# The order of the last batch's layer matrix, outputs and gates in a residual-stack kernel, and its last rows in two PSUM banks

## Chip, cores and metric

The kernel runs on one core of a Trainium2 chip. The metric is the device time of one execution in microseconds (us). Five engines work side by side and meet through semaphores: PE (TensorE, with PEld for its weight loads), DVE (VectorE), ACT (ScalarE), POOL (GpSimd) and SP (SyncE, which issues most DMAs). In the trace each engine's instructions come in the order in which the built program holds them.

## What is computed

`x` has 16 batches of 512 steps with 512 features. Four layers are added to it one after the other:

```python
x = x + L0(x, cond)   # a gate per batch: x becomes g2 * x
x = x + L1(x, cond)   # an RNN over the 512 steps
x = x + L2(x, cond)   # two sigmoid gates f, i and a candidate c; then
                      #   f, i <- f/(f+i), i/(f+i); scans along the steps
x = x + L3(x, cond)   # x @ (base + A_b B_b^T): one matrix for each batch b
```

L2 needs, for each batch, three products `x @ W` (512 x 512 each), a reciprocal, and three scans over the 512 steps. L3 needs for each batch a matrix `layer` of 512 x 512, made of a base and a product of rank 8 (with the identity of the residual folded into the base), and then the product of the batch's L2 result with it.

## The kernel before

The RNN comes first (to about 912 us of the span) and holds PE with thousands of small matmuls; in its shadow a part of the L2 gates is made early and parked in DRAM (`early`). What the change touches is the second stage, the loop over the batches `b` from line 758 on, with features on the partitions in four chunks `j`:

- `gate_unit(b, j, x3)` (L684 to L720) makes one chunk of the L2 result. PE makes `pf`, `pi`, `pc` (L684, each four matmuls 128x128 by 128x(512-te), te being the steps that were made early; the trace shows each of these float32 matmuls as two, so x8). ACT takes sigmoids of `pf` and `pi` (L699). DVE then runs ten instructions: the sum L700, the reciprocal L701, L702 to L705, the scans L709, L713 and L715, and the product L712. POOL adds the rest (L719, L720) into `x3`; for the very last chunk DVE does these two itself. PSUM holds one bank for `pf`, one for `pi`, and two for `pc` (`pc0`, `pc1`, by j). The SBUF tiles `f`, `i`, `s` have two buffers each, so ACT can write `f` of chunk j+1 only when POOL's L719 has read `f` of chunk j-1.
- `layer_of(b, ...)` makes the matrix of L3 in four banks, `pl0`, `pl1`, `po0`, `po1`: four matmuls with 8 rows (L525), and four DVE additions of the base (L529), which free the four banks. Its result goes to `wx_sb`, in the last batch to `base_sb` itself.
- `last_layer(b, x3, layer)` makes the outputs: four row tiles t, each of four matmuls 128x128 by 128x512 (L739) into `po0` or `po1` in turn, a copy by ACT (L734) and a DMA issued by SP (L735).

For b up to 14 the calls come as gates j = 0, 1, then the outputs of batch b-1, then gate j = 2, the matrix of batch b, gate j = 3. For b = 15 the matrix is called after gate j = 0, and the outputs of batch 14 after gate j = 3. Then come the outputs of batch 15: four banks `pl0`, `pl1`, `po0`, `po1` collect the chunks k = 0 to 2 first, which need no result of the last gate chunk, and then k = 3. The last row tile's bank is copied in two halves, by ACT and by DVE, which leave by two DMAs, issued by SP and ACT.

The order in this stage isn't written out by hand: the framework's scheduler places the instructions of every engine from the order of the calls and its own estimates. A tile's new owner waits until the engines that used the old one are done with it.

Of the kernel before, what the change touches and what calls it, by code (L numbers as in the profile page):

```python
# [30 lines left out]
F32 = mybir.dt.float32  # L31
# [4 lines left out]
P = 128  # L36
B, S, D = 16, 512, 512
KC = D // P
# [45 lines left out]
def kernel(  # L84
# [21 lines left out]
    nc = tc.nc  # L106
# [19 lines left out]
    base_sb = keep.tile([P, KC, D], F32)  # L126
# [387 lines left out]
    def load_layer(b, at, bt):  # L514
        for c in range(KC):
            rows = slice(c * BP, c * BP + R)
            nc.sync.dma_start(out=at[rows, :], in_=factor[0][b, :, c * P : (c + 1) * P])
            nc.sync.dma_start(out=bt[rows, :], in_=factor[1][b])
        return at, bt

    def make_layer(at, bt, banks):

        for c, pl in enumerate(banks):
            rows = slice(c * BP, c * BP + R)
            nc.tensor.matmul(pl, at[rows, :], bt[rows, :], start=True, stop=True)  # L525

    def add_base(banks, layer):
        for c, pl in enumerate(banks):
            nc.vector.tensor_tensor(layer[:, c, :], pl, base_sb[:, c, :], ALU.add)  # L529
# [25 lines left out]
    for n in range(NBLK):  # L555
# [3 lines left out]
        for s in range(T):  # L559
# [35 lines left out]
            bank, place = PLACE[g]  # L595
            for c in range(KC):
                at = slice(c * BP, (c + 1) * BP)
# [9 lines left out]
            if s == max(PAIRS[g]):  # L607
                t0, t1 = PAIRS[g]
                step = t1 - t0
                at = slice(n * T + t0, n * T + t1 + step // abs(step), step)  # L610
# [11 lines left out]
            if s in (2, 6) and n < 2 * KC:  # L622


                i = 2 * n + s // 6
                if i < 3 * KC:
                    m, which = divmod(i, 3)
                    w_sb, w = ((wf_sb, wfT), (wi_sb, wiT), (wc_sb, wcT))[which]
                    j = (KC - 2, KC - 1, 0, 1)[m]
                    at = slice(j * P, (j + 1) * P)  # L630
                    nc.scalar.dma_start(out=w_sb[:, :, at], in_=chunks(w)[:, :, at])
                else:
                    k = i - 3 * KC
# [19 lines left out]
        if n == NBLK - 4:  # L653
            at = w2pool.tile([P, P], F32, tag="b2", name="at_0", bufs=2)
# [10 lines left out]
    work = ctx.enter_context(tc.tile_pool(name="work", bufs=2))  # L665
# [9 lines left out]
    def bank(tag, name):  # L675
        return pools[tag].tile([P, D], F32, tag=tag, name=f"{tag}_{name}")
# [45 lines left out]
    def layer_rows(b):  # L722
        at = work.tile([P, P], F32, tag="at", name=f"at_{b}", bufs=1)
        bt = work.tile([P, D], F32, tag="bt", name=f"bt_{b}", bufs=1)
        return load_layer(b, at, bt)

    def layer_of(b, at, bt, layer):
        banks = [bank(tag, f"{b}_layer") for tag in ("pl0", "pl1", "po0", "po1")]
        make_layer(at, bt, banks)
        add_base(banks, layer)  # L730

    def leave(b, t, po, tag="osb"):
        osb = work.tile([P, D], F32, tag=tag, name=f"osb_{b}_{t}")
        nc.scalar.copy(osb, po)  # L734
        nc.sync.dma_start(out=out[b, t * P : (t + 1) * P, :], in_=osb)  # L735

    def output_part(po, t, x3, layer, ks):
        for k in ks:
            nc.tensor.matmul(  # L739
                po, x3[:, k, t * P : (t + 1) * P], layer[:, k, :], start=(k == 0), stop=(k == KC - 1)  # L740
            )

    def last_layer(b, x3, layer):
        for t in range(S // P):
            po = bank(f"po{t % 2}", f"{b}_{t}")
            output_part(po, t, x3, layer, range(KC))
            leave(b, t, po)

    layer = wx_sb
    pending = None  # L750
    for b in range(B):
        x3 = x3pool.tile([P, KC, S], F32, tag="x3", name=f"x3_{b}")
        end = b == B - 1
        if 0 < b < B - 1:
            factors = layer_rows(b)
        for j in range(KC):
            gate_unit(b, j, x3)
            if j == (KC - 1 if end else 1) and pending is not None:
                last_layer(*pending)
            if j == 2 and 0 < b < B - 1:  # L760
                layer_of(b, *factors, layer)
            if j == 0 and end:

                layer_of(B - 1, *layer_rows(B - 1), base_sb)
        pending = b, x3, layer

    pos = [bank(tag, "last") for tag in ("pl0", "pl1", "po0", "po1")]
    for t, po in enumerate(pos):
        output_part(po, t, x3, base_sb, range(KC - 1))
    for t, po in enumerate(pos):  # L770
        output_part(po, t, x3, base_sb, (KC - 1,))

        tag = ("osb", "f", "i", "s")[t]
        if t < KC - 1:
            leave(B - 1, t, po, tag)

    osb = work.tile([P, D], F32, tag=tag, name="osb_last")
    for n, copy in enumerate((nc.scalar.copy, nc.vector.tensor_copy)):
        at = slice(n * D // 2, (n + 1) * D // 2)
        copy(osb[:, at], pos[-1][:, at])  # L780
        (nc.sync, nc.scalar)[n].dma_start(out=out[B - 1, (KC - 1) * P :, at], in_=osb[:, at])


# [56 lines left out]
```

## Time and profile before

| | |
|---|---|
| median of 3 runs | 1621.4 us (1620.3 to 1623.64) |
| the profiled execution, its own time | 1621.03 us |
| its span, first to last instruction | 1619.2 us |
| PE busy | 1607.0 us, 99% of the span |
| DVE busy | 1132.3 us, 70% |
| ACT busy | 421.5 us, 26% |
| POOL busy | 172.9 us, 11% |
| mean granted clock of PE | 0.999 |

The page of the profile shows one execution. All times below are microseconds from the start of its span. A line of the timeline reads: start, duration, engine, line of the kernel, operation, output tile <- input tiles, shapes, count, and in brackets how long the engine stood idle before it and who released it. Tile names are shown without their numbers, so `s` or `pf` is that of whatever chunk is due at that time; the chunk is found by the order and by the width (the early part differs by chunk: for batch 15, 320 columns are left in chunks 0 and 1, 368 in chunk 2, 352 in chunk 3).

### The profile page before, as it was taken

To read this page: it belongs to the slowest core of one execution; us is meant where nothing else is said; L and a number is where in the kernel's file an instruction comes from. 1 tells how busy PE (TensorE), PEld (TensorE's weight loads), DVE (VectorE), ACT (ScalarE), POOL (GpSimd) and SP (SyncE) were. 2 spreads that over 40 slices of the span, in tenths; PEclk is the share of its full clock that TensorE was granted. 3 is DMA by queue.
4 is the path that set the end of the run, shared out by engine and by line. 5 is a ranking of instruction groups with operands and counts; after the bars stand their busy time and mean duration, and the time that the engine had idled before them with its cause. 6 is when DMAs were issued, how large, how long until landed. Compare 5 with 4: busy or idle time off the path is not lost.

```text
span 1619.2 us, 67613 instructions
## 1 busy us (share of the span) xinstructions
PE 1607.0 (99%) x29319; PEld 1147.3 (71%) x29320; DVE 1132.3 (70%) x3618; ACT 421.5 (26%) x2484; POOL 172.9 (11%) x145
## 2 busy tenths in 40 slices
PE   8999999999999999999999999999999999999998
PEld 6888888888888888888888655555555555555564
DVE  3555655665665666656665798888888888998887
ACT  3333333333333333333333211111111111111111
POOL 1000000000000000000000022221222222222212
PEclk9999999999999999999999999999999999999999
DMA  6555432111111111111111001111111111111111
GB/s 211 137 153 134 120 106 60 31 37 37 37 36 37 37 36 37 36 34 33 37 38 31 26 23 35 40 43 39 43 39 42 44 46 39 31 44 46 41 41 60
DMA packets 117683, 88.09 MB, mean 54 GB/s; under 512 B 20949, under 2 KB 97529, under 8 KB 117385
## 3 DMA queue, kind: packets, MB, share of 16 engines
q1 hardware_dynamic: 77968, 63.43, 13.0%
q10 hardware_dynamic: 39416, 20.34, 4.4%
q8 instruction: 229, 3.75, 1.0%
q14 instruction: 70, 0.57, 0.1%
HBM read 55.67 MB, written 28.07 MB: 52 GB/s over the span
## 4 chain that ended last, share of the span: by engine, by line
PE 96%; DVE 1%; DMA 1%; issue 1%; ACT 0%; POOL 0%; SPq 0%; ACTq 0%; POOLq 0%; DVEq 0%
PE pre L407 41%; PE po L739 13%; PE pg L455 13%; PE pf L684 9%; PE pi L684 9%; PE pc L684 9%; PE pf L370 1%; PE pl_layer L525 1%; DMA xb<-in_xT_dram 1%; PE po_last L739 0%; PE pl_last L739 0%; DMA wx_sb<-in_wx_dram 0%; DVE s L701 0%; POOL s L719 0%; DVE s L709 0%
## 5 line engine op out<-in xcount | busy, mean ns | idle before, releaser
L407 PEld LDWEIGHTS pre<-wh_sb,h_out 128*32 128x32 f32 x16384 | 469.2, 110 | 146.4 <-DVE h_out L599 141.7
L407 PE MATMUL pre<-wh_sb,h_out 128*32 128x128 f32 x16384 | 569.6, 273 | 3.1 <-DVE h_out L599 1.1
L599 DVE STREAM_TRANSPOSE h_out<-a 128x32 f32<-128x32 f32 x2048 | 264.7, 186 | 352.5 <-ACT a L598 351.4
L598 ACT ACTIVATE a<-pre 128x32 f32<-128x32 f32 x2048 | 238.2, 203 | 579.7 <-PE pre L407 579.5
L407 PE MATMUL pre<-wx_sb,x 128*32 128x128 f32 x8192 | 292.0, 273 | 1.2 <-DMA wx_sb<-in_wx_dram 1.1
L407 PEld LDWEIGHTS pre<-wx_sb,x 128*32 128x32 f32 x8192 | 244.3, 110 | 3.0 <-DMA wx_sb<-in_wx_dram 1.5
L739 PE MATMUL po<-wx_sb,x 128*128 128x512 f32 x480 | 208.7, 592 | 0.0
L739 PEld LDWEIGHTS po<-wx_sb,x 128*128 128x128 f32 x480 | 91.1, 190 | 111.2 <-issue 105.5
L684 PE MATMUL pf<-x,wf_sb 128*128 128x352 f32 (+3 forms) x512 | 165.5, 466 | 1.9 <-ACT f L699 1.5
L684 PE MATMUL pi<-x,wi_sb 128*128 128x352 f32 (+3 forms) x512 | 163.6, 462 | 0.0
L684 PE MATMUL pc<-x,wc_sb 128*128 128x352 f32 (+3 forms) x512 | 163.6, 462 | 0.0
L701 DVE RECIPROCAL s<-s 128x368 f32<-128x368 f32 (+2 forms) x64 | 152.2, 2378 | 2.2
L684 PEld LDWEIGHTS pf<-x,wf_sb 128*128 128x128 f32 x512 | 95.8, 190 | 70.7 <-issue 15.8
L719 POOL TENSOR_TENSOR s<-s,f 128x512 f32<-128x512 f32 x63 | 86.5, 1373 | 509.2 <-DVE s L713 509.2
L684 PEld LDWEIGHTS pi<-x,wi_sb 128*128 128x128 f32 x512 | 97.3, 190 | 55.9
L684 PEld LDWEIGHTS pc<-x,wc_sb 128*128 128x128 f32 x512 | 97.3, 190 | 55.9
L611 DVE TENSOR_TENSOR x<-x,h_out 128x128 f32<-128x128 f32 x256 | 101.2, 395 | 19.5 <-PE pg L455 0.9
L699 ACT ACTIVATE f<-pf,vec_sb 128x368 f32<-128x368 f32 (+2 forms) x64 | 35.7, 558 | 279.1 <-POOL s L719 161.1
L734 ACT COPY osb<-po 128x512 f32<-128x512 f32 x60 | 35.1, 585 | 248.5 <-DMA out_dram<-osb 109.2
L667 POOL MEMSET zero<- 128x1 f32 x1 | 0.1, 98 | 911.5 <-DMA early<-ei 911.5
L700 DVE SCALAR_TENSOR_TENSOR s<-f,i 128x368 f32<-128x368 f32 (+2 forms) x64 | 34.6, 541 | 87.6 <-ACT i L699 87.6
L455 PE MATMUL pg<-x,wf_sb 128*32 128x512 f32 (+1 forms) x640 | 86.6, 582 | 0.0
(109 smaller groups left out, 1278.2 us busy)
## 6 DMA issues: line engine op xcount, KB each, us to landing
w<-in_l3w_dram SPq DMA_DIRECT2D x68, 256.0 KB
out_dram<-osb SPq DMA_DIRECT2D x63, 256.0 KB
xb<-in_xT_dram ACTq DMA_DIRECT2D x61, 256.0 KB
early<-ef SPq DMA_DIRECT2D x19, 256.0 KB
early<-ei SPq DMA_DIRECT2D x19, 256.0 KB
f<-early SPq DMA_DIRECT2D x16, 96.0 KB
i<-early SPq DMA_DIRECT2D x16, 96.0 KB
i<-early SPq DMA_DIRECT2D x16, 80.0 KB
```

The costliest lines, as they stand in the source:

```text
L407: nc.tensor.matmul(pre[PLACE[g][0]][j * BP : (j + 1) * BP, PLACE[g][1], :], lhsT, tile_columns(w, j), start=False, stop=False, skip_group_ ...
L455: nc.tensor.matmul(ps[c * BP : (c + 1) * BP, :].rearrange("p (b t) -> p b t", **shape), w[:, k, j * P + c * BP : j * P + (c + 1) * BP], x2 ...
L598: nc.scalar.activation(a[:, at], pre[bank][:, place, at], AF.Tanh)
L599: nc.vector.transpose(turned[:, c, :], a[:, at])
L611: nc.vector.tensor_tensor(x2[:, :, :, at].rearrange("p k b t -> p k t b"), xs[n][:, :, t0 // 2, :, :], turned.rearrange("p k (t b) -> p k ...
L684: nc.tensor.matmul(p[:, te:], w_sb[:, k, j * P : (j + 1) * P], x2[:, k, b, te:], start=(k == 0), stop=(k == KC - 1),)
L699: nc.scalar.activation(gate[:, new], p[:, new], AF.Sigmoid, bias=col(bias, j))
L700: nc.vector.scalar_tensor_tensor(s[:, new], f[:, new], EPS, i[:, new], ALU.add, ALU.add)
L701: nc.vector.reciprocal(s[:, new], s[:, new])
L719: engine.tensor_tensor(s, s, f, ALU.add)
L734: nc.scalar.copy(osb, po)
L739: nc.tensor.matmul(po, x3[:, k, t * P : (t + 1) * P], layer[:, k, :], start=(k == 0), stop=(k == KC - 1))
```

## The change

In the last batch the matrix of L3 and then the outputs of batch 14 are called after gate j = 2, ahead of gate j = 3. The last row tile of the output goes to two banks with 256 columns each (`po1` and `pi`), one copied by DVE and one by ACT; both DMAs are issued by SP.

```diff
         for j in range(KC):
             gate_unit(b, j, x3)
-            if j == (KC - 1 if end else 1) and pending is not None:
+            if j == KC - 2 and end:
+                layer_of(B - 1, *layer_rows(B - 1), base_sb)
+            if j == (KC - 2 if end else 1) and pending is not None:
                 last_layer(*pending)
             if j == 2 and 0 < b < B - 1:
                 layer_of(b, *factors, layer)
-            if j == 0 and end:
-                layer_of(B - 1, *layer_rows(B - 1), base_sb)
         pending = b, x3, layer
 
-    pos = [bank(tag, "last") for tag in ("pl0", "pl1", "po0", "po1")]
+    last = S // P - 1
+    pos = [bank(tag, "last") for tag in ("pl0", "pl1", "po0")]
+    ends = [bank(tag, "end")[:, : D // 2] for tag in ("po1", "pi")]
+    columns = [slice(n * D // 2, (n + 1) * D // 2) for n in range(2)]
+
+    def last_rows(ks, n):
+        for k in ks:
+            nc.tensor.matmul(
+                ends[n],
+                x3[:, k, last * P :],
+                base_sb[:, k, columns[n]],
+                start=(k == 0),
+                stop=(k == KC - 1),
+            )
+
     for t, po in enumerate(pos):
         output_part(po, t, x3, base_sb, range(KC - 1))
+    for n in range(2):
+        last_rows(range(KC - 1), n)
+
     for t, po in enumerate(pos):
         output_part(po, t, x3, base_sb, (KC - 1,))
-
-        tag = ("osb", "f", "i", "s")[t]
-        if t < KC - 1:
-            leave(B - 1, t, po, tag)
-
-    osb = work.tile([P, D], F32, tag=tag, name="osb_last")
-    for n, copy in enumerate((nc.scalar.copy, nc.vector.tensor_copy)):
-        at = slice(n * D // 2, (n + 1) * D // 2)
-        copy(osb[:, at], pos[-1][:, at])
-        (nc.sync, nc.scalar)[n].dma_start(out=out[B - 1, (KC - 1) * P :, at], in_=osb[:, at])
+        leave(B - 1, t, po, ("osb", "f", "i")[t])
+    for n, copy in enumerate((nc.vector.tensor_copy, nc.scalar.copy)):
+        last_rows((KC - 1,), n)
+        osb = work.tile([P, D // 2], F32, tag=("s", "osb")[n], name=f"osb_end_{n}")
+        copy(osb, ends[n])
+        nc.sync.dma_start(out=out[B - 1, last * P :, columns[n]], in_=osb)
```

## The prediction

> **What bounds the kernel now.** First the page: engine shares, then the chain that ended last.
>
> ```profile
> PE 1607.0 (99%) x29319; PEld 1147.3 (71%) x29320; DVE 1132.3 (70%) x3618; ACT 421.5 (26%) x2484; POOL 172.9 (11%) x145
> ...
> PE 96%; DVE 1%; DMA 1%; issue 1%; ACT 0%; POOL 0%; SPq 0%; ACTq 0%; POOLq 0%; DVEq 0%
> ```
>
> PE is busy for 1607.0 of 1619.2 us. The change neither adds nor removes columns of matmul, so all that it can save is idle PE time. The timeline of PE over the last 80 us shows how much there is: one stall, ahead of the last chunk's gates, and the 3.51 us from PE's end (1615.69, critical chain) to the span's end.
>
> ```profile
> 1571.63 2.74 PE L684 MATMUL pf<-x,wf_sb 128*128 128x368 f32 x8
> 1574.21 2.64 PE L684 MATMUL pi<-x,wi_sb 128*128 128x368 f32 x8
> 1576.68 2.64 PE L684 MATMUL pc<-x,wc_sb 128*128 128x368 f32 x8
> 1580.84 2.63 PE L684 MATMUL pf<-x,wf_sb 128*128 128x352 f32 x8 [1.52 <-ACT f L699]
> 1583.31 2.53 PE L684 MATMUL pi<-x,wi_sb 128*128 128x352 f32 x8
> 1585.68 2.53 PE L684 MATMUL pc<-x,wc_sb 128*128 128x352 f32 x8
> 1588.05 13.90 PE L739 MATMUL po<-wx_sb,x 128*128 128x512 f32 x32
> ```
>
> The next view is the timeline of DVE, because in the last batch DVE is behind PE. From 1549.46 to 1607.8 it has no idle time, and it works on a chunk long after PE made it:
>
> ```profile
> 1569.43 0.47 DVE L700 SCALAR_TENSOR_TENSOR s<-f,i 128x320 f32<-128x320 f32 x1
> ...
> 1578.76 1.26 DVE L529 TENSOR_TENSOR base_sb<-po_layer,base_sb 128x512 f32<-128x512 f32 x2
> 1579.94 0.60 DVE L700 SCALAR_TENSOR_TENSOR s<-f,i 128x320 f32<-128x320 f32 x1
> ...
> 1588.54 0.52 DVE L700 SCALAR_TENSOR_TENSOR s<-f,i 128x368 f32<-128x368 f32 x1
> ```
>
> The three L700 lines are the starts of chunks 0, 1 and 2 of batch 15. Chunk 0, with the four base additions (L529) among it, takes 10.51 us; chunk 1, without them, 8.60 us. The two additions that free `po0` and `po1` come last, at 1578.76, though PE made the four products at 1563.28 to 1564.8 (L525): the banks stay taken for 15 us. Before the change nobody needs them then. `po` of batch 14 starts at 1588.05.
>
> **The change part by part.** In the built program PE's order after the change is: chunks 0, 1, 2 (9 groups), the four matrix products (L525), `pf` and `pi` of chunk 3, the 16 output matmuls of batch 14, `pc` of chunk 3, then the last outputs. The first output matmul now waits for DVE as well as POOL, since its bank `po0` was last held by the matrix product. In DVE's order the two L529 that free `po0` and `po1` stand behind the whole of chunk 2, after its scan L713.
>
> *PE to the new wait.* Without L525 between them, chunk 1 follows chunk 0 1.5 us sooner, but `pf` of chunk 2 can't start before 1571.63: it waits for ACT's sigmoid at 1571.05, which waits for POOL and DVE of the chunk before, and those don't change. So the 1.5 us only turn into a stall. Chunk 2 ends near 1579.2, the moved L525 take 1.5 (their old place: 1563.28 to 1564.78), to 1580.7. `pf` of chunk 3 needs DVE's chunk 0, which is now about 1.1 us sooner, so it starts at 1580.7 instead of 1580.84: the stall shown above is filled, 0.14 us gained. `pf` takes 2.5 and `pi` 2.4: PE reaches the output matmul at **1585.6**.
>
> *DVE to the release.* Chunk 0 starts at 1569.43 as before and takes 8.60 instead of 10.51, chunk 1 8.60: chunk 2 starts at 1586.63. A chunk of 368 columns with four L529 stands in the trace for batch 14: L700 at 1549.46, the first of the last two L529 at 1559.32, the next L700 at 1560.50. By that row the L529 on `po0` starts 9.86 after L700 and takes 0.67 (1.26 for the two): **1597.16**. Bounds: if removing an L529 saves its whole step (0.54, 0.58 and 1.18 us by the starts around it), 1596.8; if it saves nothing, L700 of chunk 2 at 1588.54 as now, 1599.1. I take 1597.2, by the row of a chunk without L529.
>
> *The sum.* PE stands from 1585.6 to 1597.2, some 11.6 us, with `pc` of chunk 3 (2.37 us, which needs nothing new) queued behind the waiting matmul, and the last outputs behind that. What then remains on PE is all that ran from `po` on, 13.73 + 5.15 + 5.15 + 1.72 + 1.73 = 27.48 in the critical chain, plus `pc` 2.37 = 29.85; and 0.26 for a start after a stall (2.63 for the `pf` after the stall against 2.37 for the `pi` after it). The last four DVE steps of chunk 3 (L712 to L720, with L705 3.9 us by their rows) begin when `pc` is done and lie beside 10.3 us of matmuls of k = 0 to 2. PE ends at 1597.2 + 29.85 + 0.26 = 1627.3, if its clock holds.
>
> *The clock.* The trace has no PE stall near 11.6 us, so this term is bounded by two rows. Across the stall of 1.52 us the clock stayed at 1.00: lower bound 0. In the first 20 us PE has short gaps only (0.39 us the longest from 3 to 20 us), and yet:
>
> ```profile
> 10.00:15.00 5.00, 3.61 (x85) 2.02 (x83) 2.43 (x11) 3.27 (x9) 0.00 (x0) 1.00 1.06 385
> 15.00:20.00 5.00, 4.42 (x92) 3.78 (x88) 0.98 (x6) 0.47 (x4) 0.00 (x0) 0.66 0.97 277
> ```
>
> The columns are the stretch, its length, the busy time of PE, PEld, DVE, ACT and POOL, then PE's granted clock. After 5 us in which PE was busy for 3.61, the clock fell to 0.66 in the mean: 5 x 0.34 = 1.7 us of full-speed work lost. A stall of 11.6 us is far emptier than that, and what follows it is dense matmul. I take 1.7, by this row, and twice that, 3.4, as the upper end.
>
> The Trainium skill (TensorE: Matmul & The Clock Gate, What's actually happening) has PE fall to half clock after at least one idle window of about 3.4 us and come back after at least one busy one. The row differs, since the clock fell there without such an idle window; no run here shows a stall of that length. By the page the estimate would be 3.4 to 6.8 us at half clock, a loss of 1.7 to 3.4 us, and a sum of 1633.9 to 1635.6.
>
> *The two banks.* Before, DVE's half copy (L780) starts at 1616.17, 0.02 after ACT's ends, and the last DMA is issued at 1616.63:
>
> ```profile
> 1615.77 0.37 ACT L780 COPY osb_last<-po_last 128x256 f32<-128x256 f32 x1 [0.33 <-PE po_last L739]
> 1616.16 0.33 SPq L781 DMA_DIRECT2D out_dram<-osb_last  x1
> 1616.17 0.43 DVE L780 COPY osb_last<-po_last 128x256 f32<-128x256 f32 x1 [8.34 <-ACT osb_last L780]
> 1616.63 0.37 ACTq L781 DMA_DIRECT2D out_dram<-osb_last  x1
> ```
>
> After, DVE copies one half while PE still makes the other, and the last DMA is issued when ACT is done, as SP's at 1616.16 now: 0.47 us sooner relative to PE's end (0 if SP's first issue, 0.33 us, is in the way). The 16 matmuls of 256 columns replace 8 of 512: half of 0.429 each (13.73 for 32) is 0.2145, just above the weight load's 190 ns, so they should cost nothing; if each took the 0.269 of 320 columns (2.15 for 8), 0.9 us more. I take 0, by the step from 512 to 320 columns, which is proportional.
>
> Total: PE's end moves from 1615.69 to 1629.0 (1627.3 + 1.7), that is 13.3; less 0.47 at the tail: +12.85. Against the profiled execution's own time of 1621.03 that is **1633.9 us**. This execution lies 0.4 under the median of the runs shown, so a median of 1634.3 would fit as well.
>
> **The rivals.**
>
> (a) The same stall, but the clock holds: 1632.2. For it: 1.00 in all rows from 20 us on. Against it: the longest stall of the last 80 us is 1.52, and the row of 15 to 20 us.
>
> (b) The same stall, and PE comes back at half clock for twice as long: 1635.6. It depends on where the resumption falls; nothing in the trace decides it.
>
> (c) A shorter stall. DVE's unbroken run begins at 1549.46 after 5.66 us of idling behind ACT, which was itself held by output DMAs (waits of 4.62 and 7.84 us). If these land sooner in another execution, DVE is up to 5.66 us less behind, and PE waits some 6: about 1628. Against it: the three runs differ by 3.3 us at most.
>
> (d) Not slower: the listing of the order names the engine of each wait, not the instruction that it counts to. If DVE's count at the first output matmul stood for an addition of the matrix before (batch 14, done by 1560.6), PE would go on at 1585.6 without a stall, and the change would give 0.14 + 0.47 us: 1620.4. It decides at the L529 on `po0`: done before 1585.6, no loss. Against it: the bank's last reader is this L529, and writing `po0` earlier would overwrite the matrix.
>
> **How the numbers follow.** Forecast 0.60, (a) 0.14, (b) 0.14, (c) 0.07, (d) 0.05. Lower end: (a) with DVE at its early bound, 1631.8, less 1 for a little of (c): 1630.8. Upper end: (b) with 0.9 for the narrow matmuls, 1636.5. Left out are (d), most of (c), and DVE's late bound together with (b). A difference of 0.2%, 3.2 us, is about what a measurement of this kernel can tell from no change. Slower by more than that is everything but (d): 0.95. Faster by over 0.2% isn't to be had, since all PE idle time of the end is less than that: 0.01; same 0.04.
>
> **What would show it.** In the profile after: a stall of 10 to 13 us ahead of the first `po<-wx_sb` matmul, released by DVE L529; the L525 filling the place of the old 1.52 stall; `pc` of chunk 3 behind the 16 output matmuls; DVE idle ahead of L705 in the last chunk; a clock under 1.00 in the slice after the stall; DVE's copy of the last rows ending before ACT's starts. It is wrong if the L529 on `po0` comes before PE has finished `pi`, or if `po` starts without a wait.

## The result and the profile after

The changed kernel is slower: a median of 1636.48 us over six runs (1632.79 to 1638.67) against 1623.39 us for six runs of the kernel before (1620.3 to 1625.6), a ratio of 1.0085 [1.0071, 1.0099]. Its profiled execution took 1636.38 us with a span of 1634.6 us, so the two profiled executions differ by 15.35 us where the prediction has 12.85. The two medians differ by 13.09 us; the ratio stands for 13.8.

First PE's share on the page of the changed kernel, with the chain that ended last:

```profile
PE 1608.8 (98%) x29328; PEld 1148.5 (70%) x29328; DVE 1132.6 (69%) x3618; ACT 421.3 (26%) x2484; POOL 172.6 (11%) x145
...
PE 95%; DVE 3%; DMA 1%; issue 1%; ACT 0%; SPq 0%; ACTq 0%; DVEq 0%
```

PE's busy time grew by 1.8 us for the same columns, and the span by 15.4. The rest is idle time, and DVE's share of the chain went from 1% to 3%. The timeline of PE over the end of the changed kernel shows where:

```profile
1572.55 2.74 PE L684 MATMUL pf<-x,wf_sb 128*128 128x368 f32 x8 [1.81 <-ACT f L699]
...
1577.60 2.64 PE L684 MATMUL pc<-x,wc_sb 128*128 128x368 f32 x8
1580.17 0.70 PE L525 MATMUL pl_layer<-bt,at 8*128 8x512 f32 x2
...
1581.24 2.63 PE L684 MATMUL pf<-x,wf_sb 128*128 128x352 f32 x8
1583.71 2.53 PE L684 MATMUL pi<-x,wi_sb 128*128 128x352 f32 x8
1598.12 16.94 PE L739 MATMUL po<-wx_sb,x 128*128 128x512 f32 x32 [11.88 <-DVE base_sb L529]
1614.90 2.53 PE L684 MATMUL pc<-x,wc_sb 128*128 128x352 f32 x8
```

The old stall of 1.52 us ahead of chunk 3 is gone: L525 fills it. In its place stand a stall of 1.81 us ahead of chunk 2 and one of 11.88 us ahead of the outputs of batch 14, with `pc` of chunk 3 behind them. The 32 output matmul records take 16.94 us, where they took 13.90 before. The reason for the stall is in the timeline of DVE of the changed kernel:

```profile
1587.48 0.52 DVE L700 SCALAR_TENSOR_TENSOR s<-f,i 128x368 f32<-128x368 f32 x1
...
1597.31 1.26 DVE L529 TENSOR_TENSOR base_sb<-po_layer,base_sb 128x512 f32<-128x512 f32 x2
...
1617.46 0.58 DVE L705 SCALAR_TENSOR_TENSOR i<-pc,vec_sb,i 128x352 f32<-128x352 f32 x1 [12.05 <-PE pc L684]
```

PE made the products by 1581.3, but DVE started chunk 2 only at 1587.48, and the additions that free `po0` and `po1` stand 9.83 us behind that start. Later the two engines change places: DVE stands for 12.05 us, since `pc` of chunk 3 is queued on PE behind the outputs.

The reason for the 16.94 us is in the stretches of 3 to 5 us (length, busy time of PE, PEld, DVE, ACT and POOL, PE's granted clock, DMA share, GB/s):

```profile
1587.00:1592.00 5.00, 0.00 (x0) 0.00 (x0) 4.97 (x7) 1.00 (x2) 2.73 (x2) 0.84 0.11 33
1592.00:1597.00 5.00, 0.00 (x0) 0.00 (x0) 5.00 (x7) 0.00 (x0) 0.00 (x0) 0.50 0.00 0
1597.00:1600.00 3.00, 1.88 (x3) 0.88 (x4) 2.97 (x5) 0.00 (x0) 2.45 (x2) 0.50 0.00 0
1600.00:1605.00 5.00, 5.00 (x8) 2.02 (x7) 4.90 (x6) 0.15 (x1) 0.24 (x1) 0.59 0.00 0
1605.00:1610.00 5.00, 5.00 (x13) 2.28 (x12) 0.42 (x1) 1.02 (x2) 0.00 (x0) 1.00 0.19 73
```

While PE stood, its clock fell to 0.50. It stayed there when PE went on: from 1600 to 1605, at 0.59 in the mean, 8 matmuls lie in the stretch, and 13 in the next one at full clock. The record of the clock has it at half from 1590.45 to 1604.10. PE resumed at 1598.12, so 5.98 us of matmul ran at half speed, a loss of 2.99 us.

The tail of the changed kernel in the timeline:

```profile
1630.59 0.59 PE L775 MATMUL pi_end<-base_sb,x 128*128 128x256 f32 x2
1630.86 0.42 DVE L794 COPY osb_end<-po_end 128x256 f32<-128x256 f32 x1 [9.37 <-PE po_end L775]
1631.26 0.37 ACT L794 COPY osb_end<-pi_end 128x256 f32<-128x256 f32 x1 [0.32 <-PE pi_end L775]
1631.39 0.90 SPq L795 DMA_DIRECT2D out_dram<-osb_end  x2
```

DVE's copy is done (1631.28) when ACT's has just started (1631.26), nearly as meant. Yet PE's end (1631.18) to the span's end is 3.42 us, against 3.53 before: 0.11 us gained.

### The profile page after: what moved, and what is told of

It reads as the page before. It is cut to its first block, busy times and chain, and to the rows that moved or that the text cites. A ratio compares the mean times of both kernels' runs of the same rounds, so it can differ in the third digit from the quotient of the medians.

```text
span 1634.6 us, 67633 instructions
## 1 busy us (share of the span) xinstructions
PE 1608.8 (98%) x29328; PEld 1148.5 (70%) x29328; DVE 1132.6 (69%) x3618; ACT 421.3 (26%) x2484; POOL 172.6 (11%) x145
## 4 chain that ended last, share of the span: by engine, by line
PE 95%; DVE 3%; DMA 1%; issue 1%; ACT 0%; SPq 0%; ACTq 0%; DVEq 0%
PE pre L407 41%; PE po L739 13%; PE pg L455 12%; PE pf L684 9%; PE pc L684 9%; PE pi L684 9%; PE pf L370 1%; PE pl_layer L525 1%; DVE s L701 1%; DMA xb<-in_xT_dram 1%; PE pl_last L739 0%; DMA wx_sb<-in_wx_dram 0%; DVE s L709 0%; DVE s L713 0%; PE po_last L739 0%
## 5 line engine op out<-in xcount | busy, mean ns | idle before, releaser
L739 PE MATMUL po<-wx_sb,x 128*128 128x512 f32 x480 | 211.8, 599 | 11.9 <-DVE base_sb L529 11.9
L739 PEld LDWEIGHTS po<-wx_sb,x 128*128 128x128 f32 x480 | 92.1, 192 | 125.3 <-issue 118.5
L700 DVE SCALAR_TENSOR_TENSOR s<-f,i 128x368 f32<-128x368 f32 (+2 forms) x64 | 34.6, 541 | 87.5 <-ACT i L699 87.5
```

The costliest lines, as they stand in the source:

```text
L700: nc.vector.scalar_tensor_tensor(s[:, new], f[:, new], EPS, i[:, new], ALU.add, ALU.add)
L739: nc.tensor.matmul(po, x3[:, k, t * P : (t + 1) * P], layer[:, k, :], start=(k == 0), stop=(k == KC - 1))
```

## The experiments

All ratios are against the kernel before on the same chip. "The changed kernel" is the one with the whole change.

**The matrix back in its old place**

```diff
-            if j == KC - 2 and end:
-                layer_of(B - 1, *layer_rows(B - 1), base_sb)
             if j == (KC - 2 if end else 1) and pending is not None:
                 last_layer(*pending)
             if j == 2 and 0 < b < B - 1:
                 layer_of(b, *factors, layer)
+            if j == 0 and end:
+                layer_of(B - 1, *layer_rows(B - 1), base_sb)
```

> The changed kernel with the matrix of batch 15 back after gate j = 0; the outputs of batch 14 stay ahead of gate j = 3 and the two banks stay. Theory (the wait is for the bank that the matrix took): the additions on po0 and po1 are done near 1579.4, PE reaches the outputs at 1579.2, so there is no stall of over 0.5 us ahead of them, the old stall of 1.5 us ahead of chunk 3 is filled too, and the kernel is 1.4 us faster than before (ratio 0.9991), 14 us faster than the changed one. Rival (putting the outputs ahead of the last gates is what costs, since DVE gets the last chunk late): the stall moves to the last matmuls of k = 3, which wait for DVE's L720, and the kernel stays 5 us or more slower than before.

Measured: 1620.81 us, a ratio of 0.9996 [0.9987, 1.0005]. PE in this kernel:

```profile
1570.57 2.74 PE L684 MATMUL pf<-x,wf_sb 128*128 128x368 f32 x8
...
1578.52 13.97 PE L739 MATMUL po<-wx_sb,x 128*128 128x512 f32 x32 [0.26 <-DVE base_sb L529]
1592.33 2.53 PE L684 MATMUL pf<-x,wf_sb 128*128 128x352 f32 x8
```

The wait is 0.26 us, the outputs take 13.97, and chunk 3 follows without the old stall. The last chunk of `x3` isn't late either: DVE is done with it at 1608.28, and the matmuls that read it start at 1609.74. So the loss belongs to the matrix's move. The outputs alone, moved ahead of the last gates, don't cost anything: from `pf` of chunk 2 to the span's end it is 46.2 us, against 47.6 in the kernel before (1619.2 - 1571.63). Of that gain of 1.4 us the runs can't tell more than that it is no loss.

**Only the outputs back in their old place**

```diff
-            if j == (KC - 2 if end else 1) and pending is not None:
+            if j == (KC - 1 if end else 1) and pending is not None:
                 last_layer(*pending)
```

> The changed kernel with the outputs of batch 14 back after gate j = 3; the matrix stays after gate j = 2, and the two banks stay. Theory (the matrix's move alone makes the wait): pc of chunk 3 now stands ahead of the waiting output matmul, so the stall is 2.4 us shorter (9.5 us, released by DVE L529 at the same time), the clock still falls, and the kernel is 2.4 us faster than the changed one, 10.7 us slower than before. Rival (the moved outputs make the wait): the stall goes and the kernel is within 1.5 us of before.

Measured: 1632.49 us, 1.0068 [1.0055, 1.0082].

```profile
1585.18 2.53 PE L684 MATMUL pc<-x,wc_sb 128*128 128x352 f32 x8
1597.23 15.71 PE L739 MATMUL po<-wx_sb,x 128*128 128x512 f32 x32 [9.52 <-DVE base_sb L529]
```

The matrix's move makes the wait by itself. With the outputs behind `pc` it is 2.36 us shorter, by the `pc` that now runs first: the second part of the change adds what it queues behind the waiting matmul, and no more.

**Other banks for the outputs of batch 14**

```diff
+        tags = ("pc1", "pf") if b == B - 2 else ("po0", "po1")
         for t in range(S // P):
-            po = bank(f"po{t % 2}", f"{b}_{t}")
+            po = bank(tags[t % 2], f"{b}_{t}")
```

> The changed kernel, matrix and outputs at their new places, but the outputs of batch 14 go to the banks pc1 and pf instead of po0 and po1. Theory (bank): the first output matmul waits only for DVE's L705 of chunk 1, near 1583.4 in the changed kernel's trace, a stall of 2 to 3 us instead of 11.9, with no loss of clock; PE's end comes 13 us sooner than in the changed kernel, and the time is 1 to 2 us over that of before (ratio 1.0009). Rival (the moved matrix delays DVE, and the outputs would wait for some other DVE result whatever bank they use): stall of 8 us or more, time at least 8 us over before.

Measured: 1625.96 us, 1.0024 [1.0015, 1.0034], more than the 1.0009 expected.

```profile
1582.55 3.67 PE L739 MATMUL pc<-wx_sb,x 128*128 128x512 f32 x8 [2.24 <-DVE i L705]
```

Same place of the matrix, but the outputs don't want the banks that it holds: the stall is 2.24 us, and it is now for the last reader of `pc1`, L705 of chunk 1. So the 11.88 us are the wait for two PSUM banks, and not for the matrix's result. (PE's order isn't quite the same here, since `pf` of chunk 3 needs a bank that the outputs use and comes behind them; the experiment with the banks in another order, below, keeps it.) The profiled execution, 1622.8, is the lowest of this kernel's runs; the other nine lie 2.1 to 5.7 us above it. Seven of the nine have a mean granted clock of 0.998 or 0.997 where the profiled one has 0.999, and 0.001 of the span is 1.6 us, so the clock is probably part of it; where it fell in them no trace shows.

**Work for PE while it waits.** Twelve products that nobody reads fill PE between `pi` of chunk 3 and the outputs; `between` is called in the gate unit ahead of `pc1`, so the order of the rest stays that of the changed kernel. This kernel does more than the reference asks. The main lines of the edit:

```diff
+            def between(pending=pending):
+                unread = bank("pc1", "unread")
+                for n in range(KEEP):
+                    nc.tensor.matmul(unread, x2[:, 0, 0, :P], x2[:, 0, 1, :], start=True, stop=True)
+                last_layer(*pending)
+            gate_unit(b, j, x3, between if end and j == KC - 1 else None)
```

> The changed kernel with 12 products of 128x512, which nobody reads, put between pi of chunk 3 and the outputs of batch 14 (10.3 us of PE work into pc1, which is free then). The wait for the bank is the same, to 1598 or so. Theory (clock): PE has no idle stretch over 2 us, the granted clock stays at 1.00, the 16 output matmuls take 13.9 us instead of 16.9, and the kernel is 3.0 us faster than the changed one, still 10 us slower than before. Rival (the long first stretch after the stall is a restart of the queue or of the weights, not the clock): the outputs take near 16.9 us again, and the time is that of the changed kernel.

Measured: 1633.72 us, 1.0070 [1.0057, 1.0082], which is 2.4 us under the changed kernel by the ratios (0.0015 of 1621); the two intervals overlap, so the traces have to decide. Lines below 684 are shifted here: L742 is the changed kernel's L739, L530 its L529.

```profile
1587.08 10.46 PE L763 MATMUL pc_unread<-x 128*128 128x512 f32 x24
1599.13 13.97 PE L742 MATMUL po<-wx_sb,x 128*128 128x512 f32 x32 [1.59 <-DVE base_sb L530]
...
1595.00:1600.00 5.00, 3.41 (x8) 1.25 (x7) 5.00 (x7) 0.00 (x0) 1.44 (x2) 1.00 0.00 0
```

PE was busy instead of idle, the release came no sooner (PE resumed 1.01 us later than in the changed kernel, and the whole stage runs some 1 us later here), and the outputs took 13.97 us again, with the granted clock at 1.00 in every 5 us from 1585 to 1615 (the last line is the stretch with the release). The 2.97 us between 16.94 and 13.97 are therefore the price of the clock, and what drops the clock is that PE stands.

**The matrix's banks in another order.** The matrix takes `po0`, `po1` first, so that DVE frees them first; the outputs are called between `pi` and `pc` of chunk 3 by the same device, to keep PE's order. The edit of the banks:

```diff
-        banks = [bank(tag, f"{b}_layer") for tag in ("pl0", "pl1", "po0", "po1")]
+        tags = ("po0", "po1", "pl0", "pl1") if b == B - 1 else ("pl0", "pl1", "po0", "po1")
+        banks = [bank(tag, f"{b}_layer") for tag in tags]
```

> The changed kernel with the four banks of the last matrix taken in the order po0, po1, pl0, pl1, so that DVE's additions that free po0 and po1 are the two inside chunk 2 (ends near 1591.0 and 1594.5 in the changed kernel's trace) and not the two behind it (1598.0); PE's order is that of the changed kernel. Theory (PE waits for the place of the addition in DVE's order): the stall is 4.9 us instead of 11.9, and the time is 7 us under the changed kernel by the wait, and up to 3 us more where the clock doesn't fall or comes back sooner: 8 to 10 us under it, 3 to 5 over before (ratio 1.0025). Rival (DVE as a whole is late, and the wait ends with all of chunk 2): stall near 11.9 again, time of the changed kernel.

Measured: 1629.39 us, 1.0047 [1.0032, 1.0062]. DVE, then PE, of this kernel:

```profile
1588.58 0.63 DVE L529 TENSOR_TENSOR base_sb<-po_layer,base_sb 128x512 f32<-128x512 f32 x1
1591.99 0.67 DVE L529 TENSOR_TENSOR base_sb<-po_layer,base_sb 128x512 f32<-128x512 f32 x1
```

```profile
1589.35 15.67 PE L742 MATMUL po<-wx_sb,x 128*128 128x512 f32 x32 [4.93 <-DVE base_sb L529]
```

The stall follows the addition that frees the bank, from 11.88 to 4.93 us, with everything else in place. The time came out higher than expected. Half of the excess is seen: the clock fell in this stall too, and the outputs took 15.67 us instead of 13.97, 1.7 us. The rest lies between the runs and the profiled execution, whose span (1624.5) is only 5.3 us over the 1619.2 of the kernel before. The four other runs have a mean granted clock of 0.997 where the profiled one has 0.998, some 1.6 us by these rounded values; beyond that it isn't explained.

**The changed kernel once more, beside it**

> The changed kernel once more, for the clock after its stall. Theory (the granted clock changes only on a fixed grid of 3.41 us, down after one step without matmuls and up after one step full of them): the stall is 11.9 us again, PE starts at half clock and comes back between 3.41 and 6.83 us later, so the 16 output matmuls take 15.6 to 17.4 us, another value in that range than the 16.94 seen. Rival (the loss is a constant of this stall): 16.9 us.

Measured: 1635.34 us, 1.0078 [1.0063, 1.0092].

```profile
1598.04 15.91 PE L739 MATMUL po<-wx_sb,x 128*128 128x512 f32 x32 [11.89 <-DVE base_sb L529]
```

The same kernel and the same stall to 0.01 us, but the outputs took 15.91 us and not 16.94. So the loss by the clock isn't a property of the stall's length. The six runs of the changed kernel point the same way: their mean granted clock goes from 0.994 to 0.997, and the longest (1638.67 us) has 0.994, the shortest (1632.79) 0.997. The records of the clock in the four kernels with a stall:

| kernel | PE stood | at half clock | of that with PE at work | half of it | outputs over 13.97 |
|---|---|---|---|---|---|
| changed | 1586.24 to 1598.12 | 1590.45 to 1604.10 | 5.98 | 2.99 | 2.97 |
| changed, again | 1586.15 to 1598.04 | 1588.30 to 1601.95 | 3.91 | 1.96 | 1.94 |
| outputs back | 1587.71 to 1597.23 | 1590.50 to 1600.74 | 3.51 | 1.76 | 1.74 |
| other order of banks | 1584.42 to 1589.35 | 1589.53 to 1592.94 | 3.41 | 1.70 | 1.70 |

The half-clock stretches are 13.65, 13.65, 10.24 and 3.41 us: four, four, three and one step of 3.41 us. Counting such steps back from the fall, PE was busy for 0, 1.26, 0.62 and 0.18 us of the step that ended with it. Each return came at the end of the first step that PE filled; a step that it filled to 75% (1597.28 to 1600.69, changed kernel) didn't bring it. So in these four at least one whole step was made at half speed, and up to 0.75 of one more, by where the resumption fell in a step. If that is the rule, a fall costs 1.7 to 3.4 us; the most that a run shows is 2.99.

**The tail.** Three kernels on the 0.36 us by which the tail fell short, all with the matrix in its old place. In the first, ACT issues the last DMA:

```diff
-        nc.sync.dma_start(out=out[B - 1, last * P :, columns[n]], in_=osb)
+        (nc.sync, nc.scalar)[n].dma_start(out=out[B - 1, last * P :, columns[n]], in_=osb)
```

> The first experiment's kernel (matrix back after gate j = 0), with the last DMA issued by ACT instead of SP. It is for the tail, from PE's end to the end of the span: 3.51 us in before, 3.4 in the changed kernel and in each experiment so far, where 3.04 was predicted. Theory (the transfers bound it: some 1 MB leaves in the last 3.5 us at 300 to 400 GB/s): no change, 3.3 to 3.45 us. Rival (SP issues two DMAs one after the other, 0.90 us for both): 3.1 us or less.

In the second, SP issues both, but of the row tiles 1 and 2 of the last batch only 64 of 512 columns are written, so most of these two DMAs' bytes are left out:

```diff
-        leave(B - 1, t, po, ("osb", "f", "i")[t])
+        osb = work.tile([P, D], F32, tag=("osb", "f", "i")[t], name=f"osb_last_{t}")
+        nc.scalar.copy(osb, po)
+        width = D if t == 0 else D // 8
+        nc.sync.dma_start(out=out[B - 1, t * P : (t + 1) * P, :width], in_=osb[:, :width])
```

> The first experiment's kernel, in which of row tiles 1 and 2 of the last batch only 64 of 512 columns are written to the output (the other columns of these rows are left out); copies and number of DMAs stay. Theory (the transfers bound the tail): 448 KB less at some 350 GB/s is up to 1.3 us less queue ahead of the last DMA; the last DMA then takes only its own time, and the tail falls from 3.4 to about 3.0 us, the value predicted. Rival (issue and landing bound it): 3.4 us as before.

The third has both edits, with the same columns left out:

> The kernel of the experiment with fewer bytes (row tiles 1 and 2 of the last batch written to the output in 64 of 512 columns only, the others left out), with the last DMA issued by ACT besides. With ACT's issue alone the tail was 3.46 us, with fewer bytes alone 3.29. Theory (two limits nearly equal: the DMA engines are full to the end in the one, SP's second issue comes 0.3 us late in the other): together the tail falls to 3.0 to 3.1 us, the value that was predicted. Rival (a fixed time from PE's end to the last landing, whatever is ahead): 3.3 us or more.

Measured, one run each (1617.34, 1620.32 and 1618.21 us), from PE's end to the span's end: 3.53 us before, 3.42 changed, 3.41 with the matrix back, 3.46 with ACT's issue, 3.29 with fewer bytes, 3.19 with both. In the seven traces with SP's two issues and all bytes it is 3.40 to 3.42 us, so differences of 0.1 can be told. In the run with ACT's issue:

```profile
1612.18 0.37 ACT L794 COPY osb_end<-pi_end 128x256 f32<-128x256 f32 x1 [0.32 <-PE pi_end L775]
1612.31 0.40 SPq L795 DMA_DIRECT2D out_dram<-osb_end  x1
1612.59 0.37 ACTq L795 DMA_DIRECT2D out_dram<-osb_end  x1
```

The DMA is issued 0.04 us after its copy. In the changed kernel SP's second issue starts 0.26 us after it (1631.89 against 1631.63), and its first has lasted until 1631.80. The earlier issue gains nothing. What follows PE's end (1612.10) there is, by the stretches:

```profile
1612.00:1613.00 1.00, 0.10 (x1) 0.00 (x0) 0.20 (x1) 0.37 (x1) 0.00 (x0) 1.00 0.87 330
1613.00:1614.00 1.00, 0.00 (x0) 0.00 (x0) 0.00 (x0) 0.00 (x0) 0.00 (x0) 1.00 0.97 353
1614.00:1615.00 1.00, 0.00 (x0) 0.00 (x0) 0.00 (x0) 0.00 (x0) 0.00 (x0) 1.00 0.22 79
```

The 16 DMA engines are nearly full (0.87, 0.97) while the 1 MB of the last batch leaves, from 1611.05 to 1614.32, and a DMA that is issued sooner only queues sooner: the last byte moves 2.22 us after PE's end with either issue. But the tail isn't bytes alone. From the last byte to the span's end (1615.56) nothing is moved; in all twelve traces of this document that takes 1.18 to 1.25 us. With both edits, PE's end at 1612.91 and the span's at 1616.10:

```profile
1613.00:1614.00 1.00, 0.00 (x0) 0.00 (x0) 0.01 (x1) 0.37 (x1) 0.00 (x0) 1.00 0.15 34
1614.00:1615.00 1.00, 0.00 (x0) 0.00 (x0) 0.00 (x0) 0.00 (x0) 0.00 (x0) 1.00 0.76 261
1615.00:1616.00 1.00, 0.00 (x0) 0.00 (x0) 0.00 (x0) 0.00 (x0) 0.00 (x0) 1.00 0.00 0
```

Here the engines aren't full, and what is left is the way of the last DMA: issued at 1613.39, its bytes move from 1614.36 to 1614.91. That is 0.48 us from PE's end to the issue, 0.97 to the first byte, 0.55 for the bytes and 1.18 to the end. So neither expectation for both edits held: the earlier issue gives 0.10 us where bytes are few and nothing where all of them leave, and the 3.0 to 3.1 wasn't reached because the last DMA's own way, from its issue on, is already 2.70 us.

The kernel with ACT's issue, which had the lowest time so far, was then timed against the kernel before:

> The matrix back after gate j = 0, the outputs of batch 14 ahead of gate j = 3, the last rows in two banks, the last DMA issued by ACT, timed against the kernel before. By the traces it saves the stall of 1.5 us ahead of chunk 3 less 0.26 of a new one, and 0.1 at the tail: 1.4 us, ratio 0.9991, at the edge of what the runs can tell. Rival (a new wait eats it, since DVE comes to chunk 3 1.4 us later): ratio 1.0000 or more.

Measured: 1618.58 us, 0.9978 [0.9968, 0.9988], ahead of both kernels. Its interval just touches that of the matrix back alone, [0.9987, 1.0005], from which it differs in the issuer of one DMA only.

```profile
1569.97 2.74 PE L684 MATMUL pf<-x,wf_sb 128*128 128x368 f32 x8 [0.20 <-ACT f L699]
...
1577.91 13.97 PE L739 MATMUL po<-wx_sb,x 128*128 128x512 f32 x32 [0.25 <-DVE base_sb L529]
```

From the first of these lines to the span's end it is 46.2 us, 1.4 less than in the kernel before, as with the matrix back alone; that much the trace explains. The medians differ by 4.1. In the profiled executions a further 2.1 us lies in the unchanged first part: the first output matmul past 1000 us starts at 1002.41 here, at 1002.22 in the other trace of this same kernel (the one with ACT's issue above), and at 1004.51 in the kernel before. With the matrix back alone it starts at 1002.93 in the profiled execution, and yet that kernel's ratio is 0.9996. Why the first part is shorter, and whether the rest of the gain is that, isn't settled.

## Why the prediction was right or wrong, point by point

The direction and the mechanism were right: PE waits for DVE's additions, with `pc` of chunk 3 behind, at the place named. Of the 2.50 us between 12.85 and 15.35, 0.92 are there when PE resumes (1598.12 against 1597.2), 1.25 more when it ends (33.06 us later, against 29.85 + 0.26 + 1.7), which is the clock, and 0.36 are the tail; 0.03 less lies around the span. The step of the sum that failed is the clock: it was put at 1.7 us and took 2.99. With the clock and the tail as measured the sum gives 13.5 us (clock of the second trace) to 14.5 (of the first), and the ratio of the runs 13.8. The forecast of 1633.9 us is 2.6 under the median of 1636.48 mostly for another reason: it starts from one execution of 1621.03, and the six-run median of the kernel before is 1623.39.

- *PE to the new wait.* Right. L525 filled the old stall, chunk 2 waited for ACT's sigmoid as said (1.81 us). Upstream the profiled execution was 0.92 us later (`pc` of chunk 2 at 1577.60 against 1576.68), as it was at 1005 us already: that is the unchanged part, and no step of the sum. Both traces of the changed kernel have it (that matmul starts at 1005.47 and 1005.48, against 1004.51), so it may belong to the built kernel; why stays open.
- *DVE to the release.* Right: the first L529 on `po` started 9.83 us after L700 of chunk 2 (9.86 expected), and the row of a chunk without L529 was the one to take. Less the 0.92, the release was 0.10 sooner than the sum has it; PE got there 0.28 sooner and started 0.14 after the release. The stall was 11.88 us and not 11.6, mostly because it began sooner, which moves no end.
- *What remains on PE.* Right. DVE's last steps were done at 1621.48, the matmuls that read them started at 1627.58.
- *The clock.* The mis-sized term: 1.7 taken, 2.99 measured in the profiled execution, 1.96 in another of the same kernel. The row that I took it from, 15 to 20 us of the kernel before, shows one step of 3.41 us at half clock; that is the least that a fall costs, and I used it as the middle. My bounds of 0 and 3.4 hold all four stalls. The page's estimate of 1.7 to 3.4, which stood beside the sum (the Trainium skill, TensorE: Matmul & The Clock Gate, What's actually happening), agrees with all four (1.70 to 2.99). The window of about 3.4 us is the step of 3.41; but the fall didn't need a wholly idle one, since it came after a step with PE busy for 1.26 of 3.41 us, and in the early stretch after 5 us with PE busy for 3.61.
- *The two banks.* The narrow matmuls cost nothing, as taken: six in 1.29 us, 0.215 each. The tail gave 0.11 and not 0.47. Both its ends were in the prediction, and the lower one, SP's first issue in the way, is part of the answer: the last issue starts 0.71 us after PE's end where it was 0.94, so 0.23 sooner and not 0.47. The other part, DMA engines that are full until the last byte, I had not considered.
- *The rivals.* (a) fell: the clock doesn't hold. (b), twice the loss, was nearer than the forecast in one profiled execution and further in the other. (c) fell where a trace can tell: the stall was 11.88 and 11.89 us in two executions. (d) fell, and outright: PE waits for this L529, and where it is made sooner (4.93 us of stall) or isn't in the way (2.24), PE goes sooner. The prediction's reason why a gain of over 0.2% can't be had was wrong: the stall of 1.52 and the tail of 3.51 us are 5.03, more than 3.2. The matrix back in its place came to 0.9978 in the end, though only 1.4 us of that are seen in this stage.

## What to carry to other kernels

A product's cost isn't its matmuls alone: its PSUM banks stay taken until the slower engine gets to them, so when a step is moved, ask which banks it now holds, who wants them next, and how far behind the engine that frees them is. On an engine that runs in order, move the consumer only if nothing it waits for has moved with it; here the outputs alone could move at no loss, and the matrix could not. Add the price of the clock to any PE stall of some 5 us or more (1.7 to 3.0 us here, by where it ends), and don't expect anything from an earlier last DMA while the DMA engines are full.

## What the runs showed of the hardware that was not expected

- PE's clock moves in steps of 3.41 us whose place isn't tied to the stall: stalls of 11.88 and 11.89 us of one kernel cost 2.97 and 1.94 us beyond themselves. A stall of 4.93 us still cost 1.70, and there the clock fell at 1589.53, 0.18 us *after* PE had resumed. After stalls of 1.81 and 2.24 us the traces show no fall.
- Unread matmuls in a wait cost nothing on the path that sets the end and kept the clock at 1.00.
- Two DMA issues of SP, the second waiting for a copy, take 0.86 to 0.90 us, and the second starts 0.23 to 0.26 us after its copy; ACT issued the same DMA 0.04 us after it.
- In the 2 us after PE's end the DMA engines are 87 to 98% busy at 330 to 353 GB/s, so the last byte moves 2.2 us after it; the other 1.2 us of the tail, from the last byte to the span's end, move nothing, and none of the edits shortened them.
